# A routed expert layer behind attention: six batches routed into 41 full tiles, their leftovers routed with the last two

## The chip, the core and the metric

The kernel runs on one core of a Trainium2 chip. The core has a matrix engine (TensorE; PE in the profile, its weight loads PEld), VectorE (DVE), ScalarE (ACT) and GpSimd (POOL), each with an instruction queue of its own that it works through in order, and a queue for plain transfers on SyncE (SP). [...] On-chip memory (SBUF) has 128 partitions; TensorE writes into PSUM banks. The metric is the device time of one execution in microseconds. Before the change it is 2600.77 us, the median of three runs (2599.56 to 2605.90).

## What is computed

The input x is 8 batches of 1024 tokens with 512 features, in fp32. First comes causal attention with 16 heads of 32 channels, its output projection, the residual and a layer norm. Then each token goes to one of eight experts:

```python
logits = einsum('bsd,ed->bse', x, router_w) + router_b
probs = softmax(logits); weights = max(probs); top1 = argmax(probs)
y = einsum('bsd,eod->bseo', x, expert_w) + expert_b      # of which only expert top1 is kept
out = layernorm(x + y[top1] * weights)
```

Only the chosen expert has to be computed for a token. The weights are 512 x 512 for each expert.

## The kernel before

**Attention** works on pairs (the name in the code for one batch and one group of four heads; n counts them, 32 in all), and each pair on ten units u. Beside the scores, exps and values of a unit, a unit takes one piece of filling work from a list `fill`: projections of coming pairs, and output projections of the batch before. The order of instructions is written out by hand, with no reordering after it. `maxima` runs 13 units ahead of the exps (LEAD); its rows lie in seven buffers of the pool `raw`. On GpSimd attention has one duty, `affine_select` at L622, which masks the diagonal blocks of the exps before TensorE multiplies them with V (`values`, L638). The last pair's units carry the first four output projections of the last batch. The other four, `logits_ctx` and `turn_logits` follow after attention.

**After an output projection** a token tile of 128 rows is normalized (`normalize`, L693) and written to DRAM (L697), into one of two tensors `x1_seg`, one for each half of the batches. After a batch's last tile `finish_logits` completes its router logits.

**Routing** (`route(s)`, L123) runs twice, once for batches 0 to 3 and once for 4 to 7. It yields a list of pieces, of which one is carried out at the end of each unit, or one or two at the end of each expert step. The pieces find the best expert and its weight for each of the 4096 tokens, count tokens of each expert with two matmuls (`ranks`, L162), form running sums over the 32 token tiles (`running_sums`), round each expert's count up to a whole number of 128-row tiles (`ends`), and give every token a slot. Then 32 scatters on GpSimd's queue (L214), two in a piece, each write 128 records (token number and weight) of 512 bytes into `slots` in DRAM. All write the same tensor. `fetch_records` reads the records back, `rows` makes index lists of them. Since each of eight experts may leave 127 rows empty, a half needs room for (4096 + 8 x 127) / 128 = 39 tiles, and the loop below runs over all of them, 78 in the two halves.

**The expert stage** (`class experts`, L258) takes one tile a step. Step i does, in this order:

- `fetch`: a gather on GpSimd's queue (L298) of the rows of tile i + 4 (AHEAD = 4), into one of seven buffers
- `turn`: four transposes of tile i + 1 into the single PSUM bank of `bank`, copied out by ScalarE
- `times`: for tile i a bias matmul (L328) and the products with the expert's weights (L333, eight TensorE instructions in the trace), into one of three PSUM buffers
- `store`: the scaling of tile i - 1 and its scatter to the output, on GpSimd's queue (L355)
- `norm`: the weight, the residual and the statistics of tile i on VectorE (L342 to L346), into one of three buffers `yh`

After a step come one or two entries of `later` or `pieces`. The second routing runs in this way beside the first 27 steps. The first gathers are issued at step 0, after attention and its last output projections.

Of the kernel before, what the change touches and what calls it, by code (L numbers as in the profile page):

```python
# [9 lines left out]
F32 = mybir.dt.float32  # L10
# [10 lines left out]
NSEG = 2  # L21
# [6 lines left out]
def attn_moe_kernel(ctx: ExitStack, tc: tile.TileContext, x, xT, wqT, wkT, wvT, woT, rwT, rb, ewT, eb, out):  # L28

# [15 lines left out]
    TSEG = TT // NSEG  # L45
    SEG = TSEG * P
    BSEG = B // NSEG
    NTILE = (SEG + E * (P - 1)) // P
# [34 lines left out]
    first_i = const.tile([P, NTILE], I32, name="first_i")  # L83
    nc.gpsimd.iota(first_i, pattern=[[P, NTILE]], base=0, channel_multiplier=0)
    first = const.tile([P, NTILE], F32, name="first")
# [7 lines left out]
    empty_i = const.tile([P, NTILE], I32, name="empty_i")  # L93
    nc.gpsimd.iota(empty_i, pattern=[[1, NTILE]], base=NTOK, channel_multiplier=NTILE)
    empty = const.tile([P, NTILE, 2], F32, name="empty")
# [11 lines left out]
    x1_seg = [dram.tile([SEG, D], F32, name=f"x1_{s}", tag=f"x1_{s}") for s in range(NSEG)]  # L107
    slots = [dram.tile([NTILE * P, ROW], F32, name=f"slots_{s}", tag=f"slots_{s}") for s in range(NSEG)]
    records = [t.rearrange("(j p) c -> p j c", p=P)[:, :, 0:2] for t in slots]
    for s in range(NSEG):  # L110
        nc.scalar.dma_start(out=records[s], in_=empty)
# [3 lines left out]
    rec = [None] * NSEG  # L115
    gat = [None] * NSEG
    sca = [None] * NSEG
    exp_of = [None] * NSEG
# [4 lines left out]
    def route(s):  # L123

        v = {}
        sh, sht = [P, TSEG, E], [P, NTILE, E]
        lg = logits[:, s * TSEG : (s + 1) * TSEG, :]

        def weights():
            v["top"] = top = tile3("r_top", [P, TSEG])  # L130
            nc.vector.tensor_reduce(top, lg, AX.X, ALU.max)
            v["pr"] = pr = tile3("r_pr", sh)
            nc.vector.tensor_tensor(pr, lg, top.unsqueeze(2).to_broadcast(sh), ALU.subtract)
            nc.scalar.activation(pr, pr, AF.Exp)

        def records_of_tokens():
            top, pr = v["top"], v["pr"]
            den = tile3("r_den", [P, TSEG])
            nc.vector.tensor_reduce(den, pr, AX.X, ALU.add)
            nc.vector.reciprocal(den, den)  # L140
            nc.vector.tensor_tensor(pr, pr, den.unsqueeze(2).to_broadcast(sh), ALU.mult)

            v["token"] = token = tile3(f"r_token{s}", [P, 2 * TSEG + ROW - 2])
            nc.vector.memset(token[:, 2 * TSEG :], 0.0)
            token2 = token[:, : 2 * TSEG].rearrange("p (t c) -> p t c", c=2)
            nc.vector.tensor_copy(token2[:, :, 0], tok[:, s * TSEG : (s + 1) * TSEG])
            nc.vector.tensor_reduce(top, pr, AX.X, ALU.max)
            nc.vector.tensor_copy(token2[:, :, 1], top)

        def one_hot():  # L150

            top, pr = v["top"], v["pr"]
            oh = tile3("r_oh", sh)
            nc.vector.tensor_tensor(oh, pr, top.unsqueeze(2).to_broadcast(sh), ALU.is_equal)
            nc.vector.tensor_tensor(oh, oh, rev.unsqueeze(1).to_broadcast(sh), ALU.mult)
            nc.vector.tensor_reduce(top, oh, AX.X, ALU.max)
            v["hot"] = hot = tile3("r_hot", sh)
            nc.vector.tensor_tensor(
                hot, rev.unsqueeze(1).to_broadcast(sh), top.unsqueeze(2).to_broadcast(sh), ALU.is_equal
            )  # L160

        def ranks():  # L162

            n = TSEG * E
            hot2 = v["hot"].rearrange("p t e -> p (t e)")
            ps = bank(f"rank_ps_{s}")
            nc.tensor.matmul(ps[:, :n], lhsT=before, rhs=hot2, start=True, stop=True)
            nc.tensor.matmul(ps[:, n : 2 * n], lhsT=ones, rhs=hot2, start=True, stop=True)
            both = tile3("r_both", [P, 2, TSEG, E])
            nc.vector.tensor_copy(both.rearrange("p a t e -> p (a t e)"), ps[:, : 2 * n])  # L170
            v["rank"], v["each"] = both[:, 0], both[:, 1]

        def running_sums():
            run = [tile3("r_run0", sh), tile3("r_run1", sh)]
            src, step, i = v["each"], 1, 0
            while step < TSEG:
                dst = run[i % 2]
                nc.vector.tensor_copy(dst[:, :step, :], src[:, :step, :])
                nc.vector.tensor_tensor(
                    dst[:, step:, :], src[:, step:, :], src[:, : TSEG - step, :], ALU.add  # L180
                )
                src, step, i = dst, step * 2, i + 1
            v["src"] = src

        def ends():

            cnt_i = tile3("r_cnt_i", [P, E], I32)
            nc.vector.tensor_scalar_add(cnt_i, v["src"][:, TSEG - 1, :], float(P - 1))
# [3 lines left out]
            cnt = tile3("r_cnt", [P, E])  # L192
            nc.vector.tensor_copy(cnt, cnt_i)
            v["end"] = end = tile3("r_end", [P, E])
# [58 lines left out]
        )  # L253


    AHEAD = 4

    class experts:  # L258

# [672 lines left out]
```

## Time and profile before

| What | Value |
|---|---|
| median of three runs | 2600.77 us |
| the profiled execution, and its span on the core | 2600.59 us, 2598.9 us |
| TensorE busy | 2457.4 us, 95% |
| VectorE busy | 1398.8 us, 54% |
| ScalarE busy | 1492.5 us, 57% |
| GpSimd busy | 444.0 us, 17% |
| transfers | 107.13 MB, 42 GB/s over the span |
| mean granted TensorE clock | 0.972 of full speed |

The profile page lists the busy time of each engine, the same in 40 slices of the span, the chain of work that ended last, and the costliest groups of instructions. The trace behind it gives single instructions in order of time: start and duration in us, engine, line of the kernel, operation, tile written <- tiles read, and in brackets how long the engine had been idle before and what ended that. A busy share is an average over attention and the expert stage, which have different limits. The two have to be read apart.

### The profile page before, as it was taken

Reading aid. Unit: us, or ns where it says so; the run is one execution under the profiler, and the core shown is the slowest. Engines: PE = TensorE matmul, PEld = TensorE weight load, DVE = VectorE, ACT = ScalarE, POOL = GpSimd, SP = SyncE. Lnnn points to the kernel's source line nnn. Section 1 sums busy time; section 2 is a strip of 40 time slices with the busy share of each in tenths; the row PEclk is TensorE's granted clock in tenths of the full one; section 3 lists DMA queues with packets and bytes.
Section 4 is the critical chain, followed back from the end, with each engine's and each line's share of the span. In section 5 each row is a group of like instructions: output and inputs, shape, how many; then the busy total and the mean of one; then the engine's idle time right before and its main releaser. Section 6 shows DMA issues by size and latency. Waiting matters only on the chain. (4 is left out here: it accounts for less than half of the span.)

```text
span 2598.9 us, 39902 instructions
## 1 busy us (share of the span) xinstructions
PE 2457.4 (95%) x14518; PEld 923.2 (36%) x14518; DVE 1398.8 (54%) x4390; ACT 1492.5 (57%) x2946; POOL 444.0 (17%) x772
## 2 busy tenths in 40 slices
PE   8988999999999999999999999999999978879998
PEld 3333333333333333333333333333333323334443
DVE  4544555555555556555565565555555543535555
ACT  3566776666667666676666666766666682111111
POOL 0000001100010011001013210011001011465443
PEclk9988999999999999999999999999999998999999
DMA  4001001100110011000100020001000032224332
GB/s 99 1 17 37 1 1 37 62 1 2 37 62 1 1 38 62 1 1 26 53 22 21 20 62 30 1 9 58 13 15 23 29 134 74 79 95 125 105 114 79
DMA packets 68804, 107.13 MB, mean 41 GB/s; under 512 B 27739, under 2 KB 27763, under 8 KB 68608
## 3 DMA queue, kind: packets, MB, share of 16 engines
q1 hardware_dynamic: 43392, 63.05, 7.1%
q0 software_dynamic: 14528, 41.44, 4.9%
q10 hardware_dynamic: 10688, 0.10, 0.4%
q8 instruction: 115, 1.88, 0.3%
q14 instruction: 81, 0.66, 0.1%
HBM read 66.70 MB, written 41.50 MB: 42 GB/s over the span
## 5 line engine op out<-in xcount | busy, mean ns | idle before, releaser
L618 ACT ACTIVATE p<-s 128x1024 f32<-128x1024 f32 (+1 forms) x640 | 564.4, 933 | 691.5 <-PE s L611 691.5
L554 ACT ACTIVATE raw<-raw,low 128x384 f32<-128x384 f32 (+7 forms) x1024 | 780.2, 770 | 30.0 <-DVE low L532 29.6
L532 DVE CUSTOM_DVE_ANT_0 raw<-m,wide_mask 128x512 f32<-128x512 f32 (+4 forms) x1024 | 528.0, 562 | 314.5 <-PE m L522 220.5
L622 POOL TENSOR_SCALAR_AFFINE_SELECT p<-p 128x256 f32<-128x256 f32 x512 | 199.2, 407 | 1645.5 <-ACT p L618 1645.3
L522 PE MATMUL m<-big 32*128 32x384 f32 (+4 forms) x3072 | 357.1, 537 | 4.9 <-DVE lowA L532 4.9
L611 PE MATMUL s<-big 32*128 32x512 f32 (+3 forms) x3072 | 338.5, 508 | 0.0
L638 PE MATMUL pv<-p,V 128*32 128x512 f32 (+3 forms) x3072 | 330.5, 517 | 0.7 <-POOL p L622 0.7
L532 DVE CUSTOM_DVE_ANT_0 raw<-m,wide_mask,lowA 128x448 f32<-128x448 f32 (+3 forms) x512 | 284.1, 597 | 71.3 <-PE m L522 69.1
L333 PE MATMUL y<-big,gT 128*128 x624 | 300.4, 626 | 0.0
L464 PE MATMUL ps_wq<-big 128*128 128x512 f32 x512 | 257.5, 627 | 4.9 <-DMA big<-in_wqT 4.8
L464 PE MATMUL ps_wk<-big 128*128 128x512 f32 x512 | 254.4, 621 | 2.0 <-DMA big<-in_wkT 2.0
L677 PE MATMUL o<-wo,ctx 128*128 128x512 f32 x512 | 254.0, 621 | 1.9 <-DVE l L755 1.9
L490 PE MATMUL psv<-big 128*128 128x512 f32 x512 | 251.8, 617 | 0.0
L522 PEld LDWEIGHTS m<-big 32*128 32x128 f32 x3072 | 133.9, 190 | 244.7 <-issue 85.6
L605 PE MATMUL s<-mT,ones_b 3*128 3x512 bf16 (+3 forms) x1536 | 162.1, 335 | 51.4 <-DVE lowA L532 29.2
L348 ACT ACTIVATE yrstd<-ymv,eps 128x1 f32<-128x1 f32 x78 | 23.0, 295 | 324.2 <-DVE ymv L346 317.4
L554 ACT ACTIVATION_READ_ACCUMULATOR raw<-raw,low 128x1 f32 x1024 | 200.3, 196 | 0.0
L333 PEld LDWEIGHTS y<-big,gT 128*128 128x128 f32 x624 | 116.3, 196 | 137.6 <-issue 137.6
L638 PEld LDWEIGHTS pv<-p,V 128*32 128x32 f32 x3072 | 68.3, 110 | 241.7 <-issue 177.2
L605 PEld LDWEIGHTS <-ones_b 3*128 3x128 bf16 x1536 | 47.5, 91 | 289.7 <-issue 285.7
L342 DVE SCALAR_TENSOR_TENSOR yh<-y,r_rec,g 128x512 f32<-128x512 f32 x78 | 58.6, 751 | 165.6 <-PE y L333 107.4
L611 PEld LDWEIGHTS s<-big 32*128 32x128 f32 x3072 | 144.3, 189 | 9.4
(135 smaller groups left out, 1684.7 us busy)
## 6 DMA issues: line engine op xcount, KB each, us to landing
h<-in_x SPq DMA_DIRECT2D x64, 256.0 KB, 5.1
x<-h SPq DMA_DIRECT2D x64, 256.0 KB, 2.0
big<-in_xT SPq DMA_DIRECT2D x15, 1024.0 KB, 5.1
big<-in_ewT SPq DMA_DIRECT2D x8, 1024.0 KB, 5.6
g<-x,r_gat POOLq DMA_INDIRECT x78
out<-yh,r_sca POOLq DMA_INDIRECT x78
big<-in_xT SPq DMA_DIRECT2D x4, 256.0 KB, 4.4
big<-in_wqT SPq DMA_DIRECT2D x4, 256.0 KB, 4.0
```

Source lines behind the costliest of these rows:

```text
L333: nc.tensor.matmul(y_ps, lhsT=gT[:, k, :], rhs=big[:, bass.ds(e, 1), k, :].rearrange("p a o -> p (a o)"), start=False, stop=(k == NK - 1),)
L464: nc.tensor.matmul(ps, lhsT=w_sb[name][:, k, g * P : (g + 1) * P], rhs=xT_sb[b, c][:, k, :], start=(k == 0), stop=(k == NK - 1),)
L490: lambda ps, k: nc.tensor.matmul(ps, lhsT=xT_sb[b, c][:, k, o : o + P], rhs=w_sb["wv"][:, k, :], start=(k == 0), stop=(k == NK - 1),),
L522: nc.tensor.matmul(tiles[h // 2][:, h % 2, at : at + c1 - c0], lhsT=Q[n][r, qt * P : (qt + 1) * P], rhs=K[n][r, c0:c1], start=True, stop=True,
L532: nc.vector.tensor_tensor_reduce(out=raws[n, h][:, to : to + w], in0=tiles[h // 2][:, h % 2, at : at + w], in1=wide_mask[:, 640 - w :] if ...
L554: nc.scalar.activation(a[:, to : to + w], a[:, to : to + w], AF.Exp, scale=-1.0, bias=low[n][:, qt, h : h + 1], accum_out=sums[n][:, qt, h ...
L605: nc.tensor.matmul(tiles[h // 2][:, h % 2, at : at + w], lhsT=ones_b[r, :], rhs=mT[n][r, q0 : q0 + w], start=True, stop=False,)
L611: nc.tensor.matmul(tiles[h // 2][:, h % 2, at : at + w], lhsT=K[n][r, j * P : (j + 1) * P], rhs=Q[n][r, q0 : q0 + w], start=False, stop=True,)
L618: nc.scalar.activation(p[:, :, :wide], tiles[pr][:, :, :wide], AF.Exp, scale=-1.0)
L622: nc.gpsimd.affine_select(out=p[:, :, at : at + P], in_=p[:, :, at : at + P], compare_op=ALU.is_ge, fill=0.0, base=0, pattern=[[0, 2], [1, ...
L638: nc.tensor.matmul(acc[n][h * HD : h * HD + HD, 512 - w :], lhsT=V[b, j][:, ch : ch + HD], rhs=ps[h // 2][:, h % 2, at : at + w], start=fi ...
L677: lambda ps, k: nc.tensor.matmul(ps, lhsT=ctxT[b * NG + k][:, qt * P : (qt + 1) * P], rhs=w_sb["wo"][:, k, :], start=(k == 0), stop=(k == ...
```

## The change

Batches 0 to 5 (48 token tiles, T0) are routed first. They fill exactly 41 tiles (EARLY), without padding: `ends` rounds each expert's count down to whole tiles and cuts the sum at 41. Tokens beyond an expert's full tiles get the slots behind, seven tiles of leftovers (`left_over`, `place_left_over`). Records have a third value, the expert. The second routing takes batches 6 and 7 (16 token tiles) and the seven leftover tiles, whose records it loads from `slots[0]`; its 23 token tiles need room for 30 tiles. The pieces are smaller and more: rank and total are counted in two pieces, each running sum is one. x1 is one tensor.

Gathered rows go in pairs into the buffers of `raw`, which stays allocated. AHEAD is 5, the first five gathers are issued in the last five units of attention, and the norm writes its result in place of the gathered rows. Tile 0 is transposed right after `logits_ctx`. Output projections 5 to 7 of the last batch are put ahead of expert steps 0 to 2, `turn_logits` ahead of step 3. After a step come two pieces, or one where i is a multiple of 3.

```diff
-NSEG = 2
+LATE = 2
...
-    TSEG = TT // NSEG
-    SEG = TSEG * P
-    BSEG = B // NSEG
-    NTILE = (SEG + E * (P - 1)) // P
+    T0 = TT - LATE * NQT
+    EARLY = -(-(T0 * P - E * (P - 1)) // P)
+    LEFT = T0 - EARLY
+    T1 = LATE * NQT + LEFT
+    TOKS = (T0, T1)
+    NTILE = (EARLY, (T1 * P + E * (P - 1)) // P)
+    SLOTS = (T0, NTILE[1])
...
-    x1_seg = [dram.tile([SEG, D], F32, name=f"x1_{s}", tag=f"x1_{s}") for s in range(NSEG)]
-    slots = [dram.tile([NTILE * P, ROW], F32, name=f"slots_{s}", tag=f"slots_{s}") for s in range(NSEG)]
-    records = [t.rearrange("(j p) c -> p j c", p=P)[:, :, 0:2] for t in slots]
-    for s in range(NSEG):
-        nc.scalar.dma_start(out=records[s], in_=empty)
+    x1 = dram.tile([NTOK, D], F32, name="x1")
+    slots = [dram.tile([SLOTS[s] * P, ROW], F32, name=f"slots_{s}", tag=f"slots_{s}") for s in range(2)]
+    records = [t.rearrange("(j p) c -> p j c", p=P)[:, :, 0:3] for t in slots]
+    nc.scalar.dma_start(out=records[1], in_=empty)
...
+            if s:
+                nc.sync.dma_start(out=token3[:, own:, :], in_=records[0][:, EARLY:, :])
+
+        def expert_of_token():
+
+            top, pr = v["top"], v["pr"]
+            oh = at("r_b")[:, :own]
+            nc.vector.tensor_tensor(oh, pr, top.unsqueeze(2).to_broadcast(sho), ALU.is_equal)
+            nc.vector.tensor_tensor(oh, oh, rev.unsqueeze(1).to_broadcast(sho), ALU.mult)
+            nc.vector.tensor_reduce(token3[:, :own, 2], oh, AX.X, ALU.max)
...
-        def ranks():
-
-            n = TSEG * E
-            hot2 = v["hot"].rearrange("p t e -> p (t e)")
-            ps = bank(f"rank_ps_{s}")
-            nc.tensor.matmul(ps[:, :n], lhsT=before, rhs=hot2, start=True, stop=True)
-            nc.tensor.matmul(ps[:, n : 2 * n], lhsT=ones, rhs=hot2, start=True, stop=True)
-            both = tile3("r_both", [P, 2, TSEG, E])
-            nc.vector.tensor_copy(both.rearrange("p a t e -> p (a t e)"), ps[:, : 2 * n])
-            v["rank"], v["each"] = both[:, 0], both[:, 1]
-
-        def running_sums():
-            run = [tile3("r_run0", sh), tile3("r_run1", sh)]
-            src, step, i = v["each"], 1, 0
-            while step < TSEG:
-                dst = run[i % 2]
-                nc.vector.tensor_copy(dst[:, :step, :], src[:, :step, :])
-                nc.vector.tensor_tensor(
-                    dst[:, step:, :], src[:, step:, :], src[:, : TSEG - step, :], ALU.add
-                )
-                src, step, i = dst, step * 2, i + 1
-            v["src"] = src
+        def count(name, which):
+
+            n = nt * E
+            ps = bank(f"{name}_ps_{s}")
+            nc.tensor.matmul(
+                ps[:, :n], lhsT=which, rhs=v["hot"].rearrange("p t e -> p (t e)"), start=True, stop=True
+            )
+            v[name] = at(f"r_{name}")
+            nc.vector.tensor_copy(v[name].rearrange("p t e -> p (t e)"), ps[:, :n])
+
+        def running_sum(step, src, dst):
+            src, dst = v[src], at(dst)
+            nc.vector.tensor_copy(dst[:, :step, :], src[:, :step, :])
+            nc.vector.tensor_tensor(dst[:, step:, :], src[:, step:, :], src[:, : nt - step, :], ALU.add)
+            v["src"] = dst
+
+        steps, src = [], "each"
+        for i in range(math.ceil(math.log2(nt))):
+            steps.append(lambda step=2**i, src=src, dst=("r_a", "r_b")[i % 2]: running_sum(step, src, dst))
+            src = "src"
...
+            if not s:
+                nc.vector.tensor_scalar_min(end, end, float(EARLY * P))
+            v["base"] = less("r_base", end)
...
+        def left_over():
+
+            v["full"] = full = tile3("r_full", [P, E])
+            nc.vector.tensor_tensor(full, v["end"], v["base"], ALU.subtract)
+            past = tile3("r_past", [P, E])
+            nc.vector.tensor_tensor(past, v["src"][:, nt - 1, :], full, ALU.subtract)
+            sum_up(past)
+            v["skip"] = skip = less("r_skip", past)
+            nc.vector.tensor_tensor(skip, skip, v["end"], ALU.subtract)
+            nc.vector.tensor_scalar_add(skip, skip, float(EARLY * P))
+
+        def place():
+            pos = v["src"]
+            nc.vector.tensor_tensor(pos, pos, v["each"], ALU.subtract)
+            nc.vector.tensor_tensor(pos, pos, v["rank"], ALU.add)
+
+        def place_left_over():
+            pos, over = v["src"], v["each"]
+            nc.vector.tensor_tensor(over, pos, v["full"].unsqueeze(1).to_broadcast(sh), ALU.is_ge)
+            nc.vector.tensor_tensor(over, over, v["skip"].unsqueeze(1).to_broadcast(sh), ALU.mult)
+            nc.vector.tensor_tensor(pos, pos, over, ALU.add)
...
-        def scatter(t0):
-            for t in range(t0, t0 + 2):
+        def scatter(t0, t1):
+            for t in range(t0, min(t1, nt)):
...
-            [weights, wait, records_of_tokens, one_hot, ranks, running_sums, ends, slot_of_each]
-            + [lambda t0=t0: scatter(t0) for t0 in range(0, TSEG, 2)]
-            + [experts_of_tiles, wait, wait, wait, fetch_records, wait, wait, wait, rows]
+            [weights, wait, records_of_tokens, expert_of_token, wait, one_hot, wait]
+            + [lambda: count("rank", before), lambda: count("each", ones)]
+            + steps + [ends]
+            + ([] if s else [left_over])
+            + [place]
+            + ([] if s else [place_left_over])
+            + [slot_of_each, experts_of_tiles]
+            + [lambda t=t: scatter(t, t + 2) for t in range(0, nt, 2)]
+            + [wait, fetch_records, wait, rows]
         )
 
 
-    AHEAD = 4
+    AHEAD = 5
...
+        def __init__(self, raw):
+            self.raw = raw
+            self.got, self.turned, self.y, self.normed = {}, {}, {}, {}
+            self.todo = [(s, j) for s in range(2) for j in range(NTILE[s])]
...
-            self.gp, self.fp, bp = pool("gather", AHEAD + 3), pool("ffn", 3), pool("bias", 1)
+            self.fp, bp = pool("ffn", 4), pool("bias", 1)
...
-        def step(self, todo, i):
-            if i == 0:
-                for a in range(AHEAD):
-                    self.fetch(*todo[a])
-                self.turn(*todo[0])
-            if i + AHEAD < len(todo):
-                self.fetch(*todo[i + AHEAD])
+
+        def step(self, i):
+            todo = self.todo
+            self.fetch(i + AHEAD)
...
-        def fetch(self, s, j):
-            g = self.gp.tile([P, D], F32, tag="g", name=f"g_{s}_{j}")
+        def fetch(self, i):
+            if i >= len(self.todo):
+                return
+            s, j = self.todo[i]
+            if i % 2 == 0:
+                self.pair = self.raw.tile([P, 2, D], F32, tag="raw", name=f"g_{s}_{j}")
+            g = self.pair[:, i % 2]
             nc.gpsimd.indirect_dma_start(
                 out=g,
                 out_offset=None,
-                in_=x1_seg[s][:, :],
+                in_=x1[: NTOK if s else T0 * P, :],
                 in_offset=bass.IndirectOffsetOnAxis(ap=gat[s][:, j : j + 1], axis=0),
-                bounds_check=SEG - 1,
+                bounds_check=(NTOK if s else T0 * P) - 1,
...
-            (g, _), y_ps = self.got.pop((s, j)), self.y.pop((s, j))
-            h = self.fp.tile([P, D], F32, tag="y", name=f"yh_{s}_{j}")
-            nc.vector.scalar_tensor_tensor(h, y_ps, rec[s][:, j, 1:2], g, ALU.mult, ALU.add)
+            (h, _), y_ps = self.got.pop((s, j)), self.y.pop((s, j))
+            nc.vector.scalar_tensor_tensor(h, y_ps, rec[s][:, j, 1:2], h, ALU.mult, ALU.add)
...
+            raw = pool("raw", NRAW)
             st2 = ExitStack()
             pool2 = lambda name, bufs: st2.enter_context(tc.tile_pool(name=name, bufs=bufs))
-            vp, prob, raw = pool2("v", 1), pool2("prob", 4), pool2("raw", NRAW)
+            vp, prob = pool2("v", 1), pool2("prob", 4)
...
-                s, ts = divmod(t, TSEG)
-                nc.sync.dma_start(out=x1_seg[s][ts * P : (ts + 1) * P, :], in_=h)
+                nc.sync.dma_start(out=x1[t * P : (t + 1) * P, :], in_=h)
...
-                if (b + 1) % BSEG == 0:
-                    pieces.extend(route(b // BSEG))
+                if b in (B - LATE - 1, B - 1):
+                    pieces.extend(route(b // (B - 1)))
...
+                    if n == NP - 1 and u > NU - 1 - AHEAD:
+                        assert not pieces and not rows_todo
+                        moe.fetch(u - NU + AHEAD)
...
-            moe = experts(st)
+            moe.prepare(st)
             for c in range(NC):
                 logits_ctx(B - 1, c, pair_bank)
-            for qt in range(HALF, NQT):
-                run_all(output(B - 1, qt, pair_bank))
-                if later:
-                    later.pop(0)()
-            turn_logits(B - 1, pair_bank)
+            moe.turn(*moe.todo[0])
+            run_all(output(B - 1, HALF, pair_bank))
             assert not ewT_todo
 
-            todo = [(s, j) for s in range(NSEG) for j in range(NTILE)]
-            for i in range(len(todo)):
-                assert i + AHEAD != NTILE or not pieces
-                moe.step(todo, i)
-                for _ in range(2 if i < NQT or i > NTILE - 2 * NQT else 1):
+            for i in range(len(moe.todo) + 1):
+                qt = HALF + 1 + i
+                if qt < NQT:
+                    run_all(output(B - 1, qt, pair_bank))
+                if qt == NQT:
+                    turn_logits(B - 1, pair_bank)
+                assert i + AHEAD != EARLY or not pieces
+                moe.step(i)
+                for _ in range(2 if i % 3 else 1):
                     if later or pieces:
                         (later or pieces).pop(0)()
-            moe.step(todo, len(todo))
 
     with tc.manual_schedule():
         attention()
```

## The prediction

> **What bounds the kernel now.** I read the chain of waits first. It is of no use here: it holds only the last 7 us, since nothing before them is recorded as a wait. So I went by the busy table of the 40 slices and then by stages. TensorE is busy 9 tenths or more in nearly every slice up to the end of attention (2172.7 us, the first `logits_ctx` matmul of the last batch), so attention is TensorE's. Behind it come the expert tiles. Cut at points read from the timeline (columns: stretch, length, busy us of each engine with instruction counts, granted TensorE clock, DMA share, GB/s), the end of the kernel is:
>
> ```profile
> 2172.70:2203.30 30.60, 22.57 (x78) 10.62 (x76) 12.57 (x26) 0.58 (x1) 6.28 (x7) 0.86 0.43 132
> 2203.30:2223.60 20.30, 20.30 (x53) 8.97 (x52) 9.79 (x23) 6.47 (x11) 6.19 (x7) 0.87 0.37 120
> 2223.60:2246.20 22.60, 20.05 (x53) 8.78 (x52) 18.05 (x58) 3.10 (x7) 6.07 (x7) 0.92 0.19 59
> 2246.20:2344.80 98.60, 74.87 (x192) 31.80 (x192) 36.10 (x78) 11.63 (x31) 58.78 (x58) 0.91 0.27 89
> 2349.80:2586.60 236.80, 236.08 (x698) 108.63 (x698) 126.61 (x272) 41.50 (x108) 111.27 (x108) 1.00 0.35 111
> 2586.60:2598.90 12.30, 4.01 (x10) 1.52 (x9) 4.67 (x10) 0.59 (x2) 1.95 (x2) 0.82 0.01 1
> ```
>
> Row five has TensorE busy 236.08 of 236.80 us: there a tile costs what TensorE needs. The bias matmul opens each tile's products, and two of them lie one tile apart (timeline, columns: start, duration, instruction):
>
> ```profile
> 2442.34 0.38 PE L328 MATMUL y<-bias,bias_ones 3*128 x1
> ...
> 2446.73 0.38 PE L328 MATMUL y<-bias,bias_ones 3*128 x1
> ```
>
> So one tile is 4.39 us (4.385 over several). In row four, the second routing's scatters, TensorE is idle a quarter of the time. One round of GpSimd's queue there:
>
> ```profile
> 2279.63 1.06 POOL L298 DMA_INDIRECT g<-x,r_gat  x1 [0.30 <-issue]
> ...
> 2281.00 1.01 POOL L355 DMA_INDIRECT out<-yh,r_sca  x1 [0.31 <-issue]
> ...
> 2282.31 0.98 POOL L214 DMA_INDIRECT slots<-r_token,r_slot_i  x1 [0.30 <-issue]
> ...
> 2284.83 0.98 POOL L214 DMA_INDIRECT slots<-r_token,r_slot_i  x1 [1.53 <-DMA slots<-r_token,r_slot_i]
> ...
> 2286.11 1.06 POOL L298 DMA_INDIRECT g<-x,r_gat  x1 [0.30 <-issue]
> ```
>
> Gather, store and two scatters fill 6.48 us with no gap but the fixed 0.3 and the wait of each second scatter for the first one's landing. GpSimd is the bound here, not TensorE.
>
> **1. Fewer tiles.** T0 = 48 token tiles are routed early; EARLY = (48x128 - 8x127)/128 rounded up = 41 whole tiles, 7 left over; late 16 + 7 = 23, giving (23x128 + 8x127)/128 = 30. That makes 71 tiles against 78. Each one taken away lies in the row-five regime: 7 x 4.385 = **-30.7 us**. This is arithmetic on shapes and holds for any routing.
>
> **2. The junction.** Now: 30.6 us from the first `logits_ctx` to the bias matmul of tile 0, of which TensorE works 22.57, and tile 4's bias at 2223.6. After: tile 0 is gathered in attention's last five units, its transposes follow `logits_ctx`, and outputs 5, 6, 7 lie inside steps 0, 1, 2. I lay it out from the same starting point: `logits_ctx` to 2175.5, first transposes 1.1 us, output 4 to 2180.3. Output 5 must wait for a PSUM buffer until VectorE reads it at 2181.1 (behind the bias splitting, which isn't changed). Then output 5 (8 x 0.43 = 3.43 at full clock) and 0.55 of transposes: tile 0 at 2185.4. Four steps of 4.385, two outputs of 3.43, `turn_logits` 1.85 put tile 4 at 2211.7, **-12 us**. The gather wait (5.4 us idle, below) and the slow first tile (6.98 instead of 4.39 us, granted clock 0.87) are in it.
>
> ```profile
> 2200.43 1.12 PE L319 MATMUL gT_ps<-ident,g 128*128 128x128 f32 x4 [5.39 <-DMA g<-x,r_gat]
> ```
>
> The five gathers cost GpSimd 5 x 1.36 us where it idles up to 8 us between masks; they stand at a unit's end, ahead of the next unit's masks, whose exps take longer. I cost them at 0; without that cover it is 5 x 1.4 = 7 us.
>
> **3. Routing on the expert stage.** Row three: tiles 4 to 8 take 24.0 us (2223.62 to 2247.64) instead of 17.5, so 6.5 us go to the second routing, mostly while TensorE's one bank waits for VectorE (r_both) and the rank matmuls wait for the one-hot. After, ranks and totals are two pieces with an empty one before them, of 184 instead of 256 columns. Each still holds the bank until VectorE, behind the tile's norm (1.6 us), has copied it: about 1.8 us each, 4 us in all, **-2.5 us**. Bounds: 0 to 6.5 us.
>
> **4. The scatters on the expert stage.** Now: tile 8 at 2247.6, tile 24 at 2354.7: 107 us for 16 tiles of 70.2, so 36.9 are lost. After: 23 scatters instead of 32. I count the pieces: normalizing ends in step 4, scatters start in step 16 and take 4, 4, 2, 4, 4, 2, 3 per step. In GpSimd's queue a step is gather 1.36 + store 1.31 + first scatter 1.28 + 2.52 for each further one. From tile 16 (=0, the store ready at 2.8) the gather of step 23 starts at 69.5 us. A gather lands 3.54 after it starts (2255.08, transposes 2258.62), the bias matmul follows 0.57 later. AHEAD = 5 makes that gather tile 28's, which is transposed in step 27: step 27 at 73.6 instead of 11 x 4.385 = 48.2, a loss of 25.4, and about 2 for the clock after the last stall: 27, **-10 us**. In-place results take away the second brake of today, the norm that waits for the store three tiles back:
>
> ```profile
> DVE yh L342 <- DMA out<-yh,r_sca: 58.2, 15, 8.6
> ```
>
> Its 58.2 us are not added: they lie on the same GpSimd rounds. Gone, the gather is late next, already counted. Bounds: 12 us (all slack of the buffers usable, step 16 entered with GpSimd idle) to 40 (my count, applied to today, gives 29 rather than 37, so it may be a third too low).
>
> **5. Attention.** The early routing moves from batch 4 to batches 6 and 7 and grows. Starts of pairs (a batch's four heads) read at the mask-row copies (L580): its third pair takes 69.56 us with the setup, against 65.4 in batch 5 without; the fourth 66.61 against 63.93; the next first pair 68.37 against 67.79. So setup costs 4.1 and 16 scatter pieces 3.3 us (0.2 each), though a piece of two scatters holds GpSimd 5.04 us: a unit lasts 6.5 to 7 us and leaves it free. After: VectorE's setup rises from 14 to about 24 us (384 columns for 256, six running sums, the left-over steps), spread over 21 units instead of 8, so I take 6 (4 to 8). Of the 24 pieces, 17 fall on long units, 3.4 us. Seven fall on the second-last pair, which has no projections: it takes 44.5 us, 4.5 a unit, less than 5.04. Laid over today's masks, GpSimd is 3.5 us late at the mask of unit 6 (2119.6) and catches up in units 7 to 9. There ScalarE is the bound (busy 4.50 and 4.44 of two 4.5 us stretches), so I take 2 us (0 to 8). Sum 11.4 against 7.4: **+4 us**. The record fetch waits for the last scatter (2130) and lands 5.5 us later; rows() waits for it on VectorE, whose next urgent work is at 2143; nothing.
>
> A rule of the skill speaks against this part: "SBUF — State Buffer", section on the two separate sides, says that descriptors of DMAs issued on the GpSimd queue cannot be written while VectorE runs fp32 copies that take both ports. More scatters beside a busy VectorE would then lengthen. The row: the 32 scatters in attention, beside a VectorE busy 66.54 of 120 us, take 970/978/1190 ns (min/median/max); in the expert stage, VectorE busy 36.10 of 98.6 us, 977/983/997. One in 32 is 0.2 us longer. By the rule, with one 0.69 us VectorE copy waited out per scatter, the seven short units would overrun by 14 x 0.69 = 9.7 us more, and the saving fall from 51 to about 42. I take the row.
>
> **Else.** The left-over records' load (128 x 7 x 12 bytes on the SP queue, step 6) has 8 us until the one-hot of step 8; today's 4992-piece record load lands in 5.5 us. x1 in one tensor could tie writes and gathers together: at worst 2 us each, inside the gathers' 14 us of slack. Nothing.
>
> **Sum.** -30.7 - 12 - 2.5 - 10 + 4 = -51.2. From the span of 2598.9: 2547.7. The profiled execution took 2600.59 us, 1.7 outside the span; 2549.4. Its distance to the median of 2600.77 is 0.2. **Forecast 2549.5 us.**
>
> **Rivals.**
> - *Scatters hide less*: four in a row cost as the 40 us bound, and the bank waits stay at 6.5. 2549.5 + 13 + 2.5 = **2565**. For: my count is low for today. Against: in-place results and one more gather ahead.
> - *Scatters hide nearly wholly* (12 us), attention pays nothing extra: 2549.5 - 15 - 4 = **2531**. Against: 68 us of GpSimd work in seven steps of 30.7.
> - *Attention's masks queue behind the scatters*: the saving without attention is 55; 24 pieces break even at 55/24 = 2.3 us plus today's 0.2. At 3.0 us a piece (the values matmuls stand 60% of a piece) the cost is 72 - 3.3: **2614**, slower. For: two scatters stand ahead of the next masks in program order. Against: 16 such pieces cost 0.2 each; it would need the short units' behaviour in the long ones.
> - *The tiles do not fall away*: excluded, the loop runs over 41 + 30.
>
> **Chances.** Forecast's neighbourhood (2537 to 2560) 0.64; hide less 0.18; hide wholly 0.11; slower by over 0.3% 0.05; within 0.3% (what measurements of this kernel can't tell from no change) 0.02. Range 2532 to 2567: both neighbours in, the mask case out.
>
> **What will show it.** 71 bias matmuls 4.385 us apart outside the scatters; tile 0's near 2189 and no 5 us gather wait; pair 31 ending within 10 us of today's 2172.7; scatters 1.28 + 2.52 in GpSimd's queue, TensorE waiting for gathers around tiles 22 to 27 only; no wait of a norm for a store. It is wrong if attention grows by over 12 us, or if the stall spreads past tile 28.

## The result and the profile after

The changed kernel takes 2571.59 us, median of four runs (2569.9 to 2574.1), against 2600.16 (2596.29 to 2605.9) for the kernel before: ratio 0.9889, 95% interval 0.9869 to 0.9910. That is 28.6 us less; 51 were forecast, and 2571.59 lies above the range. The profiled span is 2572.3 us. The end of the kernel, cut at the first `logits_ctx` matmul (2186.35), at the bias matmuls of tiles 0, 4 and 70, and at 2301.80 and 2364.80, some 6 us ahead of those of tiles 21 and 28 (columns as before: stretch, length, busy us of PE, PEld, DVE, ACT, POOL, clock, DMA share, GB/s):

```profile
2186.35:2200.95 14.60, 12.02 (x46) 5.15 (x38) 6.42 (x13) 0.59 (x1) 2.69 (x3) 0.88 0.55 184
2200.95:2227.10 26.15, 26.15 (x85) 12.94 (x85) 13.67 (x31) 4.51 (x8) 7.33 (x7) 1.00 0.29 100
...
2301.80:2364.80 63.00, 42.65 (x101) 18.56 (x100) 15.65 (x33) 5.71 (x14) 33.19 (x33) 0.82 0.28 81
2364.80:2554.60 189.80, 189.80 (x555) 87.23 (x554) 101.47 (x219) 33.10 (x86) 89.97 (x87) 0.99 0.35 115
2554.60:2572.30 17.70, 3.99 (x10) 1.50 (x9) 4.68 (x10) 0.59 (x2) 1.97 (x2) 0.76 0.01 0
```

The first row was 30.6 us long before: tile 0 now starts 14.6 us behind attention. The third row shown is the second scatters: TensorE still idles a third of it. The fourth is again TensorE's without a gap. The fifth, the end, is 5.4 us longer than before (12.3), with the same work in it. And attention ends at 2186.35 instead of 2172.68. As a sum, each line read in both traces at the same instructions:

| Part | forecast | measured | how measured |
|---|---|---|---|
| seven tiles | -30.7 | -30.7 | 71 bias matmuls for 78, 4.385 us apart where nothing stalls |
| junction, to tile 4 | -12 | -10.2 | 30.65 + 20.29 before, 14.61 + 26.14 after |
| routing setup, expert stage | -2.5 | -0.3 | two steps of 6.6 and 8.3 us for 4.385: 6.2 lost; 6.5 before |
| scatters, expert stage | -10 | -4.6 | steps 21 to 27 lose 32.3; 36.9 before |
| attention | +4 | +13.7 | 2172.68 to 2186.35 |
| end | 0 | +5.4 | last bias matmul to end, 12.31 to 17.73 |
| sum | -51.2 | -26.7 | span 2598.9 to 2572.3 |

**Attention** lost its time in one place. Between the mask-row copies of its pairs, counted from 0, pair 30 takes 56.5 us instead of 44.5 and pair 31 2.0 us more (to `logits_ctx`); in the rest the setup that batch 4 is rid of (7) and the one that batches 6 and 7 now carry (7) cancel. Of the 12 us in pair 30, 7.4 are idle time of TensorE; the other 4.6 it works longer (35.91 us for 31.31), at a mean granted clock of 0.84 for 0.96. In pair 30 the timeline shows what GpSimd and the SP queue do (columns: start, duration, instruction, and in brackets the idle time ahead of it and what ended that):

```profile
2083.57 3.08 SPq L444 DMA_DIRECT2D big<-in_ewT  x4
...
2092.21 0.98 POOL L252 DMA_INDIRECT slots<-r_token,r_slot_i  x1 [4.17 <-DMA slots<-r_token,r_slot_i]
...
2098.52 0.98 POOL L252 DMA_INDIRECT slots<-r_token,r_slot_i  x1 [5.33 <-ACT raw L602]
2099.52 0.77 POOL L670 TENSOR_SCALAR_AFFINE_SELECT p<-p 128x256 f32<-128x256 f32 x2
...
2099.99 2.27 PE L686 MATMUL pv<-p,V 128*32 128x512 f32 x8 [5.63 <-POOL p L670]
```

L444 is the load of four experts' weights, 4 MB; a fifth follows at 2090.49. While they run a scatter waits 4.17 and 5.33 us, and 3.86 at 2104.15, instead of 1.54 for the one before to land; the masks (L670) stand behind the scatter, and TensorE behind the masks. The bracket of the second scatter names ScalarE, the release that the profile saw last; that it too waited for a landing is read from the order of the queue and from the window below (columns as above):

```profile
2090.00:2095.00 5.00, 4.11 (x30) 1.19 (x28) 4.32 (x13) 5.00 (x13) 0.98 (x1) 1.00 1.04 383
2095.00:2100.00 5.00, 0.01 (x2) 0.01 (x2) 0.00 (x0) 4.17 (x10) 1.46 (x3) 0.61 1.05 403
```

DMA share 1.05, 403 GB/s, and TensorE works 0.01 of 5 us. In the page the group of these matmuls waited 0.7 us for masks over the whole execution before (L638), and 12.5 after (L686):

```profile
L638 PE MATMUL pv<-p,V 128*32 128x512 f32 (+3 forms) x3072 | 330.5, 517 | 0.7 <-POOL p L622 0.7
...
L686 PE MATMUL pv<-p,V 128*32 128x512 f32 (+3 forms) x3072 | 331.7, 517 | 12.5 <-POOL p L670 12.5
```

### The profile page after: what moved, and what is told of

Read it like the earlier page. It is cut to its first block, busy times and chain, and to the rows that moved or that the text cites. A ratio compares the mean times of both kernels' runs of the same rounds, so it can differ in the third digit from the quotient of the medians.

```text
span 2572.3 us, 39590 instructions
## 1 busy us (share of the span) xinstructions
PE 2424.5 (94%) x14427; PEld 910.2 (35%) x14427; DVE 1385.4 (54%) x4376; ACT 1488.6 (58%) x2932; POOL 438.5 (17%) x765
## 5 line engine op out<-in xcount | busy, mean ns | idle before, releaser
L670 POOL TENSOR_SCALAR_AFFINE_SELECT p<-p 128x256 f32<-128x256 f32 x512 | 199.9, 409 | 1629.7 <-ACT p L666 1629.5
L686 PE MATMUL pv<-p,V 128*32 128x512 f32 (+3 forms) x3072 | 331.7, 517 | 12.5 <-POOL p L670 12.5
L381 PE MATMUL y<-big,gT 128*128 x568 | 272.8, 625 | 0.0
L653 PE MATMUL s<-mT,ones_b 3*128 3x512 bf16 (+3 forms) x1536 | 162.1, 335 | 51.1 <-DVE lowA L580 29.4
L686 PEld LDWEIGHTS pv<-p,V 128*32 128x32 f32 x3072 | 69.2, 110 | 253.0 <-issue 175.2
L381 PEld LDWEIGHTS y<-big,gT 128*128 128x128 f32 x568 | 106.0, 197 | 125.0 <-issue 125.0
L653 PEld LDWEIGHTS <-ones_b 3*128 3x128 bf16 x1536 | 47.3, 91 | 290.2 <-issue 286.3
L512 PEld LDWEIGHTS ps_wq<-big 128*128 128x128 f32 x512 | 88.6, 192 | 157.8 <-issue 151.9
```

Source lines behind the costliest of these rows:

```text
L381: nc.tensor.matmul(y_ps, lhsT=gT[:, k, :], rhs=big[:, bass.ds(e, 1), k, :].rearrange("p a o -> p (a o)"), start=False, stop=(k == NK - 1),)
L512: nc.tensor.matmul(ps, lhsT=w_sb[name][:, k, g * P : (g + 1) * P], rhs=xT_sb[b, c][:, k, :], start=(k == 0), stop=(k == NK - 1),)
L653: nc.tensor.matmul(tiles[h // 2][:, h % 2, at : at + w], lhsT=ones_b[r, :], rhs=mT[n][r, q0 : q0 + w], start=True, stop=False,)
L670: nc.gpsimd.affine_select(out=p[:, :, at : at + P], in_=p[:, :, at : at + P], compare_op=ALU.is_ge, fill=0.0, base=0, pattern=[[0, 2], [1, ...
L686: nc.tensor.matmul(acc[n][h * HD : h * HD + HD, 512 - w :], lhsT=V[b, j][:, ch : ch + HD], rhs=ps[h // 2][:, h % 2, at : at + w], start=fi ...
```

## The experiments

All are edits of the changed kernel. A kernel's executions differ by some us, most visibly in attention, where pairs that no edit touches take 63.9 or 65.4 us from run to run. So each theory is read from its own stage, with the median beside it, and in brackets the ratio to the kernel before with its 95% interval. Only runs 3, 8 to 11 and 13 lie clear of the changed kernel's interval; what the others gain or lose is shown in their stage alone, from one trace each. "Loss" is a step's time over 4.385 us.

**1. Are the weight loads the cause in pair 30?** They are issued at the first unit of pair 31 instead of the ninth of pair 29. The fifth load, at the end of pair 29, stays.

```diff
-            free_at = {(NP - 4, 0): [2], (NP - 3, 8): [0, 1, 3, 4]}
+            free_at = {(NP - 4, 0): [2], (NP - 1, 0): [0, 1, 3, 4]}
```

> The four expert weight loads (4 MB) that stand at the ninth unit of pair 29 are moved to the first unit of pair 31, behind the scatters. Theory A, the loads fill the transfer engines, the scatters of pair 30 land late, and the masks queued behind them stop TensorE: pair 30 falls from 56.5 us to 46 to 50, the mask wait of 5.6 us goes, the kernel is 6 to 10 us faster than the changed one (about 2564). Theory B, two scatters in a row fill GpSimd in units of 4.5 us whatever the transfers do: pair 30 stays above 54 us, the kernel within 2 us of 2571.6.

2565.1 us (0.9862, 0.9846 to 0.9879). Pair 30 takes 48.84 instead of 56.51 us, pair 31 is unchanged (44.35 to `logits_ctx`, 44.29 without the edit). The same stretch of time in this kernel:

```profile
2095.00:2100.00 5.00, 3.51 (x46) 1.54 (x40) 3.06 (x11) 4.43 (x10) 2.72 (x4) 1.00 0.22 79
```

The collision is 7.7 us of the 12, the slow stretch behind the stall included: the mean granted clock over the pair is 0.92, for 0.84 without the edit. The other traces agree: with the four loads in place and scatters beside them pair 30 takes 55.5 to 59.8 us, with the loads moved 48.1 to 52.3. What is left, 4.3 over the 44.53 of before, is the queue itself and what the fifth load, issued at 2086.11, still adds; one scatter waits almost as long as before:

```profile
2092.14 0.98 POOL L252 DMA_INDIRECT slots<-r_token,r_slot_i  x1 [3.77 <-DMA slots<-r_token,r_slot_i]
```

**2. No scatters in pair 30 at all.** Routing's pieces go two to a unit until the scatters begin, so that all fall on long units.

```diff
-                    if pieces:
-                        pieces.pop(0)()
+                    for _ in range(2 if len(pieces) > T0 // 2 + 4 else 1):
+                        if pieces:
+                            pieces.pop(0)()
```

> Two routing pieces a unit until the scatters are reached, so that the 24 scatter pieces end in pair 29, before the short pair 30 and mostly before the weight loads. A and B both: pair 30 goes back to 44 to 46 us, pairs 26 to 29 lose at most 3 us more than now, the kernel is 9 to 13 us faster (about 2561). Theory C, attention's growth comes from VectorE's longer setup: the setup is now denser, so the loss stays (within 2 us of 2571.6) and only moves to pairs 26 and 27.

2571.53 us (0.9881, 0.9861 to 0.9902). Pair 30 falls to 43.31 with the loads in their old place, so its whole excess came with the scatters: 56.51 - 48.84 = 7.7 by the four loads beside them, 48.84 - 43.31 = 5.5 by the queue, the fifth load in it. But the denser setup lengthens pairs 26 and 27 from 64.58 and 68.2 to 73.07 and 72.84: there TensorE works 7.3 us longer, at a granted clock of 0.95 and 0.93 instead of 1.00, and idles 5.9 us more, most of it for VectorE (L653: 11.1 us for 5.4). The loss has only moved.

**3. The second routing's scatters one at a time.**

```diff
-            + [lambda t=t: scatter(t, t + 2) for t in range(0, nt, 2)]
+            + [lambda t=t: scatter(t, t + 2 - s) for t in range(0, nt, 2 - s)]
```

> In the second routing each scatter is a piece of its own, so 14 expert steps take 2, 2, 1 scatters instead of seven steps with 4, 4, 2. Theory D, GpSimd's queue is the bound: per step 2.67 + 1.28 + 2.52 for each further scatter, less the slack of gathers five tiles ahead: the loss of 32 us in the scatter steps falls to 5 to 10, the kernel is 22 to 27 us faster (about 2547). Rival E, the loss belongs to 23 scatters and their traffic beside gathers and stores however they are dealt out: it falls by less than 8 us.

2554.04 us (0.9815, 0.9799 to 0.9832). The loss falls from 32.3 us to 19.0, by more than the rival's 8, and moves to steps 27 to 34. It was not the 5 to 10 us expected: 6.2 us of it, step 33, are not GpSimd's queue but the wait that run 9 shows.

**4. The counts of the second routing in a bank of their own.**

```diff
-            ps = bank(f"{name}_ps_{s}")
+            ps = ps_v.tile([P, 512], F32, tag="pv", name=f"{name}_ps_{s}") if s else bank(f"{name}_ps_{s}")
```

> The two counts of the second routing write to the PSUM bank that attention's values no longer use, instead of the single bank of the transposes. Theory F, the 6.2 us lost around tiles 10 and 11 are the transposes waiting for that bank: 4 to 6 us faster (about 2566.5), steps 10 and 11 back to 4.9 us. Rival G, TensorE waits there for the one-hot on VectorE, or for a slow clock: less than 2 us.

2566.68 us (0.9861, 0.9838 to 0.9885). Steps 9 and 10 lose 0.3 us each instead of 2.2 and 3.9. In the changed kernel:

```profile
2255.11 0.66 PE L367 MATMUL gT_ps<-ident,g 128*128 128x128 f32 x4 [1.71 <-DVE r_rank L181]
2255.70 0.38 PE L376 MATMUL y<-bias,bias_ones 3*128 x1
2256.01 5.40 PE L381 MATMUL y<-big,gT 128*128 x8
```

The wait of 1.7 us is what the forecast had. The products behind one of the two waits take 5.40 us instead of 3.70; with the bank free no products are slow. That 1.7 is the missing part, and it is the clock: in the changed kernel the granted clock is 0.50 from 2256.54 to 2259.95, which is 3.41 us at half speed. It does not follow every such wait: in run 5 both waits of 1.71 us are there, the clock stays at 1.00, and both products take 3.70. Pair 30 took 59.8 us in this execution, at a granted clock of 0.73, and hides part of the gain in the span.

**5. The constants of the expert stage behind the last logits** (`moe.prepare` two lines down).

```diff
-            moe.prepare(st)
             for c in range(NC):
                 logits_ctx(B - 1, c, pair_bank)
+            moe.prepare(st)
```

> The fetch of the six small constants of the expert stage and their casts are issued behind the last logits instead of ahead of them. Theory G (VectorE sits in these casts when the first gate product comes, PE o then waits 2.6 us for l L802): no such wait, the first bias product some 12.5 us behind the first last-logits product (14.6 in the changed kernel), 2568 to 2570 us. Theory H (the gathers of the first tiles and the slow clock set the start of tile 0): first bias product as far behind as before within 1 us, 2571 to 2573 us.

2571.09 us (0.9891, 0.9871 to 0.9911). TensorE no longer waits for VectorE at L802 (2.58 us before this edit), and tile 0 starts 10.19 us behind `logits_ctx` instead of 14.61: 4.4 us, more than expected, since the products behind that wait were slow too (5.26 us for 3.70). The median doesn't show it; the executions spread from 2561.46 to 2573.3, so what it is worth alone stays unsettled.

**6. Results in a tile of their own.**

```diff
-            (h, _), y_ps = self.got.pop((s, j)), self.y.pop((s, j))
-            nc.vector.scalar_tensor_tensor(h, y_ps, rec[s][:, j, 1:2], h, ALU.mult, ALU.add)
+            (g, _), y_ps = self.got.pop((s, j)), self.y.pop((s, j))
+            h = self.fp.tile([P, D], F32, tag="y", bufs=3, name=f"yh_{s}_{j}")
+            nc.vector.scalar_tensor_tensor(h, y_ps, rec[s][:, j, 1:2], g, ALU.mult, ALU.add)
```

> The result of a tile goes into a tile of its own, as before the change, instead of into the gathered row. Theory I (the in-place step costs nothing in the expert stage): tile steps at 4.38 us as in the changed kernel and 2570 to 2573 us. Theory J (a gather into a row's buffer now waits for the store of that buffer, and this also is what makes the program's end longer): time from the last bias product to the end 12 to 13 us instead of 17.7, 2565 to 2567 us.

2579.4 us (0.9911, 0.9880 to 0.9941). Neither: the end stays at 17.73 us, and steps 21 to 27 lose 36.5 instead of 32.3. In six other traces that leave these steps alone they lose 31.9 to 34.3, so writing in place saves 2 to 5 us on the scatters, and the long end comes from elsewhere.

**7. Seven scatters more** (of the second routing, each with the data it has already written).

```diff
             + [lambda t=t: scatter(t, t + 2) for t in range(0, nt, 2)]
+            + ([lambda t=t: scatter(t, t + 1) for t in range(7)] if s else [])
```

> Seven scatters of the second routing are issued a second time with the same data, so that GpSimd issues as many DMAs as in the kernel before (220 instead of 213). Theory K (the time of the last GpSimd drain depends on the count of its DMAs): time from the last bias product to the end about 12.3 us instead of 17.7; with the seven scatters' own cost on the expert stage (0.8 us each, 6 us) 2571 to 2573 us. Theory J (it comes from something else in the change): end stays at 17.7 us, 2576 to 2579 us.

2567.62 us (0.9879, 0.9852 to 0.9907), with 7 DMAs more than the changed kernel. The end shrinks from 17.73 to 12.08 us. The last two GpSimd instructions of the changed kernel, whose span ends at 2572.3:

```profile
2557.76 0.98 POOL L402 DMA_INDIRECT out<-g,r_sca  x1 [3.40 <-DVE g L401]
2561.71 0.98 POOL L402 DMA_INDIRECT out<-g,r_sca  x1 [2.96 <-DVE g L401]
```

and of this one, whose span ends at 2564.1:

```profile
2555.20 0.98 POOL L403 DMA_INDIRECT out<-g,r_sca  x1 [3.40 <-DVE g L402]
2560.65 0.98 POOL L403 DMA_INDIRECT out<-g,r_sca  x1 [4.47 <-issue]
```

**8. The four edits 1, 3, 4 and 5 together.**

> Weight loads later, second routing's scatters in pieces of one, its counts in another bank, constants behind the last logits, all together. If the four losses are separate: 2571.6 - 6.5 - 17.5 - 5 - 2 = about 2541 us. If the loads' later start only moves the loss to the expert stage or the single scatters already take away what the bank did: 2547 to 2554 us.

2545.08 us (0.9791, 0.9772 to 0.9810). Each loss falls as it did in runs 1, 3, 4 and 5: pair 30 48.05 us, tile 0 10.19 behind `logits_ctx`, steps 9 and 10 lose 0.3 each, steps 27 to 34 17.8. The end is 17.77.

**9. With these four, eight tiles ahead** (AHEAD = 8).

> The kernel with the four edits together, with gathers eight tiles ahead instead of five. Theory D (the scatters' remaining stall, 17.8 us on steps 27 to 34, is GpSimd's queue outrun, so three more gathered tiles of slack, 3 x 4.38 us, take most of it): excess of these steps 3 to 8 us, span 8 to 13 us below that of the four edits, less what three more gathers cost ahead of the masks in pair 31 (0 to 5). The rival: what stalls is a gather that waits for its slots' records or its buffer, which no earlier start helps; excess 15 to 18 us and the same time.

2542.57 us (0.9770, 0.9741 to 0.9798). Steps 27 to 32 lose nothing, so GpSimd's queue was the cause there. But step 33 alone loses 14.5, and the sum of the steps hardly moves, 17.8 to 15.7, as the rival had it. VectorE's timeline, and TensorE's next work behind it:

```profile
2343.93 0.18 DVE L393 BATCH_NORM_AGGREGATE ymv<-ystats 128x2 f32<-128x6 f32 x1
2361.60 0.18 DVE L279 CAST r_sca<-r_rec 128x30 int32<-128x30 f32 x1 [17.49 <-DMA r_rec<-slots]
2361.70 0.17 DVE L281 TENSOR_SCALAR r_gat<-r_rec 128x30 int32<-128x30 f32 x1
2361.78 0.15 DVE L400 RECIPROCAL yrstd<-yrstd 128x1 f32<-128x1 f32 x1
...
2364.98 1.12 PE L367 MATMUL gT_ps<-ident,g 128*128 128x128 f32 x4 [13.84 <-ACT gT L369]
```

VectorE reads the records for the index lists as soon as the piece comes up, stands there until they have landed, and a tile's norm stands behind it; ScalarE's copy of the next transposes stands behind the norm, and TensorE behind the copy. Five tiles ahead, the same wait of VectorE was 10.9 us in run 8, and TensorE stood 5.50 us behind the copy: that is the 6.2 us of step 33, in run 3 as well (5.54).

**10. and 11. Seven gathers issued twice, then three** (with the four edits; tiles 48, 50 and so on; the edit of run 10, in run 11 the range ends at 53).

```diff
-            nc.gpsimd.indirect_dma_start(
+            for _ in range(2 if i in range(48, 61, 2) else 1):
+                nc.gpsimd.indirect_dma_start(
```

> The kernel with the four edits together, and seven gathers of the late expert stage (every second tile from 48 on) issued twice: 220 GpSimd DMAs instead of 213. Theory K (count of the DMAs sets the end, whatever they are): last bias product to end about 12.1 us instead of 17.8; the rest unchanged but for at most 2 us. Rival (it was the second scatters' place or kind that shortened the end): 17.8 us stays.

> As with seven more gathers, but three: 216 DMAs. If what counts is the number modulo 4 or 8 (220 is a multiple of 4, 213 is not): end at about 12.1 us. If it is modulo 16 (220 leaves 12, 213 leaves 5, 216 leaves 8) or a size of its own: between 12 and 18 us, or 17.8 us.

Seven: 2541.69 us (0.9757, 0.9721 to 0.9794), end 12.05. Three: 2541.75 us (0.9769, 0.9744 to 0.9795), end 17.94. So the kind doesn't matter and the number does: with 220 DMAs the program ends 3.4 us behind the start of the last one (four traces, before among them), with 213 and 216 it ends 10.6 and 10.85 us behind it. Which numbers are short ones isn't settled by three of them, nor why.

**12. The read of the records later, in the changed kernel.**

```diff
-            + [wait, fetch_records, wait, rows]
+            + [wait, fetch_records] + [wait] * (9 * s + 1) + [rows]
```

> The changed kernel with nine more empty pieces between the second routing's fetch of records and VectorE's two reads of them (L279, L281), some five tiles later. Theory L (of the 32.3 us on steps 21 to 27 the last part, steps 26 and 27 with 8.3, is VectorE standing 10.3 us at L279 for the records, a tile's norm behind it): these two steps' excess falls to 0 to 3 us, the others stay at 24, span 5 to 8 us lower at 2564 to 2567. Theory D alone (all of it is GpSimd's queue, the read waits beside it): steps 26 and 27 stay above 6 us and 2570 to 2573 us.

2575.23 us (0.9899, 0.9874 to 0.9924). Steps 26 and 27 still lose 8.3 us. VectorE no longer waits at L279, yet nothing is gained: in the changed kernel TensorE stands in step 26 for a gather, with this edit or without, and the read lies beside that. It becomes a cause when the scatters come one at a time, as in runs 3 and 8, and more so with the larger slack of run 9.

**13. All of it**: the four edits, seven doubled gathers, seven tiles ahead, two pieces a step in steps 0 to 17, four empty pieces ahead of the read.

> The four edits, the seven doubled gathers (end 12.1 us), gathers seven tiles ahead, the second routing's setup two pieces per tile in steps 0 to 17 so that its scatters end some 3.6 tiles sooner, and four more empty pieces before VectorE reads the records. If queue slack and the read of the records are the two parts of the 17.8 us on steps 27 to 34: 0 to 4 us there, about 2541.7 - 15 = 2527 us. If the denser setup costs what it did in attention (bank or clock stalls) or the scatters still outrun the slack: 2532 to 2540 us.

2537.1 us, median of five (0.9758, 0.9737 to 0.9778), the lowest median, but by its ratio no faster than run 10. Steps 27 to 34 lose 2.5 instead of 17.8 us, as expected; steps 8 and 9 lose 4.4 with the denser setup. The end is 20.53: the last store still starts 3.4 us ahead of the end, but 17.1 us behind the last bias matmul, for 8.6 in run 10. Why the stores come so late here isn't shown.

## Why the prediction was too low

The 24.5 us that separate forecast and measurement are 9.7 in attention, 5.4 in the end, 5.4 in the scatters, 2.2 in the setup and 1.8 in the junction.

**Tiles: right.** -30.7, seven times a step that both traces show.

**Junction: right in kind.** Tile 0 was expected 12.7 us behind `logits_ctx` and came at 14.6, tile 4 at 40.8 for 39.0. The step said that output 5 waits for VectorE's read behind the bias splitting; that wait is the 2.58 us at L802, and run 5 shows it goes with the constants moved. It laid out 3.43 us for output 5 behind the wait, at full clock:

```profile
2195.32 5.26 PE L725 MATMUL o<-wo,ctx 128*128 128x512 f32 x8 [2.58 <-DVE l L802]
```

The granted clock is 0.50 from 2195.10 to 2198.51. In run 7, after a wait of 2.26 us, it stays at 1.00, these products take 3.70, and tiles 0 and 4 come at 12.7 and 38.9, as forecast.

**Routing setup: mis-sized**, 4 for 6.2. "About 1.8 us each" for the bank was measured at 1.7 us of waiting and 2.2 of each step; what was left out is that products behind such a wait can be slow (5.40 for 3.70 us, at half the clock), which cost 1.7 more in one of the two. Run 4 removes all but 0.6.

**Scatters: mis-sized**, 27 for 32.3. The working laid GpSimd's queue out from tile 16 (2285.94) and put the gather of tile 28 at 69.5 us behind it; it came at 2359.16, 73.2 behind. The first scatter starts at 2290.91, 0.9 later than worked out; three scatters, each 16 DMAs behind the one before it, wait 2.03 or 2.04 instead of 1.54 us:

```profile
2296.44 0.98 POOL L252 DMA_INDIRECT slots<-r_token,r_slot_i  x1 [2.03 <-DMA slots<-r_token,r_slot_i]
2298.97 0.98 POOL L252 DMA_INDIRECT slots<-r_token,r_slot_i  x1 [1.54 <-DMA slots<-r_token,r_slot_i]
```

and one store waits 1.1 us longer for VectorE. Together 3.4 of the 3.7; most of the rest of the 5.3 is a slower restart of TensorE: 1.02 us from the transposes to tile 27's bias matmul for 0.57, and 2.5 us lost behind it for 2. So the mechanism held, the end of the stall too (step 27), and the norm's wait for a store, 58.2 us before, is gone. The note that the count might run low was right: scaled by its own 37 to 29, 27 would have been 34.

**Attention: the failed step.** "Seven fall on the second-last pair ... so I take 2 us (0 to 8)" laid the scatters over the masks, each waiting 1.54 us for the one before. It didn't ask what else is on the DMA engines then. The four weight loads, issued just ahead of that pair, move their data in it. Before the change no scatter stood there, and they cost nothing: 44.53 us with them, and 43.31 in run 2. The queue is at most 5.5 us by run 2, inside the bounds; the loads' 7.7 were in no bound and no rival. The forecast's own sign, attention longer by over 12 us, came true (13.7). The rule of the Trainium skill that was weighed, "SBUF — State Buffer", section "SBUF: two separate sides", on VectorE copies and GpSimd's descriptors, isn't what happened: the scatters' own duration stays at 0.98 us in pair 30, and it is their landing that is late. Another place would have warned: the Trainium skill, "DMA: Bandwidth & Descriptors", section "Latency and other measured facts", gives an access to HBM 0.2 us on average and 2 us at high load. On the quiet wait of 1.54 that makes an estimate of 3.3 us beside the load; measured were 3.9 to 5.3. No run separates the full DMA engines from a slower memory behind them.

**The five gathers**, costed at 0, stand ahead of pair 31's masks: TensorE waits 1.87 us there for 0.69 before, and the pair is 2.0 us longer. Runs 5 and 7, with the same order, have the same wait and take 42.0 us, since the granted clock over the pair is 1.00, for 0.94 in the changed kernel and 0.96 before. So the gathers cost 1.2 us and the clock the rest.

**The end**, not in the sum at all, is 5.4 us. Runs 7 and 10 give it back, by nothing but seven more DMAs; why the number counts stays open.

The rival "scatters hide less" named 2565, nearer the result, but in part by luck: its bank waits of 6.5 came true (6.2), its scatters of 40 did not (32.3), and attention was at +4. The slower rival had the right mechanism, masks behind scatters, but for all pieces; it was real only where the unit is short and the DMA engines are full.

## What to carry to other kernels

When a DMA moves to another place, lay out who else uses the DMA engines there: a wait for a landing that is read in a quiet stretch doesn't hold beside a bulk load, and an in-order queue hands the delay to everything behind it. Count pieces that hold an in-order engine by the spacing they need, and spread them (one at a time took 13.3 us off their stage here). After each stall removed look again for the next waiter in the same stretch: behind the gathers stood the read of the records. And a wait can cost more than its length: look at the granted clock behind it.

## What had not been expected of the hardware

- Between its last DMA's start and the end of the program the core takes 3.4 us with 220 GpSimd DMAs and 10.6 to 10.85 with 213 or 216, whatever their kind.
- The wait for a scatter to land, 1.54 us in most places, is 4.17 and 5.33 us beside loads at 383 to 403 GB/s.
- With the second routing's scatters in pairs, three scatters, 16 DMAs apart, wait 2.03 or 2.04 us, in the changed kernel and in runs 1, 2, 4 to 7 and 12. In the kernel before no scatter of the second routing does, so it is no general period.
- After a wait of 1.7 us the granted clock was 0.50 for 3.41 us in the changed kernel, and stayed at 1.00 after the same wait in run 5.
